# Four graph layers on one core: who writes the edge payload, when partial sums are added, and where masks and table rows are stored

## The chip, the cores and the metric

The kernel runs on one core of a Trainium2 chip. The core has five engines with a queue of instructions each: PE (TensorE, matrix products; its weight loads are listed as PEld), DVE (VectorE), ACT (ScalarE), POOL (GpSimd) and SP (SyncE, which here only issues DMAs). Sixteen DMA engines move data between the core's memory (SBUF, and PSUM for PE's results) and the chip's main memory. The metric is the device time of one launch in microseconds (us), as the median of the runs.

## The reference

The input is 3125 nodes with 32 features, 103,125 directed edges (50,000 pairs both ways and one loop per node, sorted by target), and two vectors per edge. Four layers, each with a layer norm and a ReLU ahead of it and its input added behind it, are applied in turn:

- L0: attention over the edges with four heads, where the softmax of each source node subtracts that source's maximum over its edges;
- L1: two mean aggregations with dense weights;
- L2: a mixture of three Gaussians of the edges' two-vectors;
- L3: a spline network, which takes most of the time and is what the change is about.

```python
def spline_conv(x, row, col, basis, idx, W, b):
    N = x.shape[0]
    Fout = W.shape[2]
    z = jnp.einsum('ni,kio->nko', x, W).reshape(N * K, Fout)
    gathered = z[col[:, None] * K + idx]
    msg = jnp.einsum('es,eso->eo', basis, gathered)
    out = jax.ops.segment_sum(msg, row, num_segments=N)
    deg = jax.ops.segment_sum(jnp.ones_like(msg[:, 0]), row, num_segments=N)
    return out / jnp.maximum(deg, 1.0)[:, None] + b
...
h = jnp.ones((N, 1), x.dtype)
h = jax.nn.elu(spline_conv(h, row, col, basis, idx, stn1_w, stn1_b))
h = jax.nn.elu(spline_conv(h, row, col, basis, idx, stn2_w, stn2_b))
h = jax.nn.elu(h @ stn3_w + stn3_b)
t = h @ stn4_w + stn4_b
new_pseudo = jnp.clip(pseudo + t[col] - t[row], 0.0, 1.0)
basis2, idx2 = spline_basis(new_pseudo)
return spline_conv(x, row, col, basis2, idx2, conv_w, conv_b)
```

There are K = 125 weight matrices in a 5 x 5 x 5 grid, and each edge takes the eight corners of the cell that its three-vector falls into, with eight weights. The first spline layer has an input of ones, so it needs only each source node's sum of corner weights for the 125 grid points. L0 needs, for its maximum and its softmax, the number of edges between each source and each target: a table of counts of 3200 by 3200, mostly zeros.

## The kernel before

**Tiles of edges.** Nodes come in 25 chunks of 128. Edges are put into tiles of 128 edges with sources of one chunk; 24 chunks have 35 tiles each, the last has 15, so there are 855. As the input is sorted by target, tile k of any chunk holds a narrow window of target chunks. The 24 tiles of one k form a unit, and units form groups (`Places`, L884). The line `cuts` (L932) cuts the 35 units into eight groups: 0-2, 2-5, 5-10, 10-15, 15-20, 20-25, 25-29, 29-35. A group has a `need` (the number of input tiles after which it is complete), a `hi` (the last target chunk it reaches) and the flag `counted` (L935): counted groups have their edges counted in the edge stage, the others later, beside the gathers. Of the eight, the first six are counted and the last two are not.

**Edge stage.** The input's 806 tiles are read in 31 blocks of 26. `put_edges` (L1554) loads a block's fields (`flds`), has VectorE compute the payload of each edge (`pay`: 8 fields, the corner weights at L1207 to L1211, the 125 grid weights with the product at L1579, and a column of ones), with two copies by ScalarE (L1562 for the fields, L1583 for the ones), and then has POOL issue 26 indirect DMAs (L1585), each of which scatters 128 payload rows to their places in a table in main memory, `tab`. `pay` has three buffers.

Once a group's rows have landed, its steps run (`group_steps`, L1638, and `add_tiles`, L1596): every third step loads the tiles of three sources back (`tt`, SyncE), and each step is one source of the group: a one-hot of the sources by VectorE (L1374), one matmul per tile into the accumulator `acc1` (L1626), and the addition to `sums` by VectorE (L1628; the first time a copy by ScalarE, L1631). In a counted group, `count_edges` (L1482) then makes a one-hot of the targets per tile by VectorE (`od`, L1381, four buffers), multiplies with the sources' one-hot on PE (`cn`, L1496), and adds what an earlier group left in a column (`carry`, L1512 on VectorE; L1514, a copy by ScalarE, where there is none). Columns that are final go to `a_s`, are stored to `as_d` by SyncE (L1520), turned on PE (L1527), copied by ScalarE (L1528) and stored to `at_d` (L1529). At a group's end its narrow fields (`nar`, one buffer) are stored and its table rows computed.

A loop over the blocks sets the order of the trace: the payload of a block, then a quota of steps of the groups that have come due two blocks after their `need`. What is left after the last block runs one group after the other.

**First gather stage** (L1824 to L1858). For each of 25 chunks: the hidden features (`ps` L1841, `hid`), their transposed copy `hts`, and `spline_rows` (L1432), which makes the chunk's rows of the table z2: 16 pairs of matmuls (`z_ps` L1445, three PSUM buffers), copied into `slab` by ScalarE (L1457 and L1459) and stored by SyncE, four stores a chunk (L1461). Then the groups whose `hi` is this chunk are gathered (`summed_rows`, L1679): per source a one-hot, and per tile one indirect DMA by POOL (L1690, six buffers `g`), a product with the eight corner weights by VectorE (`prod`, L1694), and a matmul into `acc` (L1695, one PSUM buffer). After a source's last tile, VectorE adds the eight corners up (L1702) and adds the result to the total (L1703).

Beside this, `beside` runs steps of another generator, `node_steps` (L1719): each source grants 0.8 us per tile to it, and a step has a price written by hand. It counts the groups that were not counted, the last chunk's edges, prepares L0, and finds the maximum: for each third of the targets and each source chunk it loads the counts (`cnt`, SyncE, L1801), has ScalarE turn them into a mask `off` (L1803: a large number where there is no edge) and has VectorE take four maxima (L1806); `cnt` and `off` have two buffers each. When a pool of buffers is opened over memory that earlier pools used, its tiles wait until those pools are done.

**After that** come L0's attention, L1, L2, the new weights (the np stage) and the **last gather stage** with a second table z3, which uses the same `spline_rows` and `summed_rows`, with the first slab slot copied by VectorE (L1457), two accumulators and nothing beside.

Instructions of one engine are put in order by a scheduler that goes by priorities; `keep_in_program_order` adds an order edge from the instruction traced before it on that engine, and no wait.

## Time and profile before

The times below are of the device; the profiled execution is one run apart from the three.

| what | value |
|---|---|
| runs | 7129.87, 7144.23, 7144.03 us, median 7144.03 |
| profiled execution | 7107.32 us, its span 7105.1 us, mean granted TensorE clock 0.748 |
| busy in the span | PE 61%, PEld 32%, DVE 62%, ACT 23%, POOL 40% |
| stages in the span | places of edges to 170 us; scatters to 1634; remaining add steps to 1830; first gather at 1914.6, first gather stage to 3775; L0 to 4610, L1 to 4790, L2 to 5370, np to 5680; last gather stage to 7105 |
| gathers (L1690) | 1710, POOL 1921.3 us busy, 1124 ns mean |
| scatters (L1585) | 806, POOL 894.2 us busy, 1109 ns mean |
| payload product (L1579) | 5676 to 5704 ns on VectorE, one per block |

A row of a waits view names the waiting engine and its line, then the engine and line that released it, the total, the number of waits and the longest. In a view by stretch each engine has its busy time and the number of its instructions in brackets, followed by the granted clock, the DMA engines' busy share and their rate.

### The profile page before, as it was taken

The page shows a single profiled execution, that of the slowest core. Times are in us where ns is not written, and L with a number is a line of the kernel's source. Part 1 is how long each engine was busy: PE and PEld are TensorE (multiplying, and loading weights), DVE is VectorE, ACT ScalarE, POOL GpSimd, SP SyncE. Part 2 cuts the span into 40 slices and gives each one's busy share as a digit, 9 for nine tenths or more (in the row PEclk, how much of TensorE's full clock was granted, in tenths as well). Part 3 has the DMA queues.
Part 4 walks back from the last instruction along what each step waited for, and adds up shares of the span by engine and source line. Part 5 has one row for each costly group of instructions (what it writes and reads, how often), then busy time and mean ns, then how long its engine had stood idle before and what let it go on. Part 6 is the DMA issues. An engine that isn't in the chain of part 4 may idle for free. (4 is left out here: it accounts for less than half of the span.)

```text
span 7105.1 us, 67076 instructions
## 1 busy us (share of the span) xinstructions
PE 4311.1 (61%) x20956; PEld 2240.6 (32%) x20956; DVE 4426.9 (62%) x8893; ACT 1661.1 (23%) x2860; POOL 2826.5 (40%) x2541
## 2 busy tenths in 40 slices
PE   4023134136788877776777777756775499654445
PEld 1012023125433323222222222255664433333333
DVE  5325255256486686779668989818998955444444
ACT  0012022023424223321205878701110022000000
POOL 0775754741153553646571000000000035677776
PEclk5555566568899787878898999977885556677776
DMA  3123233235698886977864433361114478655543
GB/s 100 51 80 93 73 105 108 76 106 166 253 343 316 310 297 242 366 268 269 332 223 151 119 116 120 107 218 60 54 54 179 147 292 300 200 160 157 156 142 101
DMA packets 524310, 1245.13 MB, mean 175 GB/s; under 512 B 271284, under 2 KB 334463, under 8 KB 510886
## 3 DMA queue, kind: packets, MB, share of 16 engines
q0 software_dynamic: 148912, 613.60, 26.2%
q1 hardware_dynamic: 357974, 613.44, 25.5%
q10 hardware_dynamic: 17056, 13.70, 0.6%
q8 instruction: 168, 2.75, 0.2%
q14 instruction: 200, 1.64, 0.1%
HBM read 907.51 MB, written 366.91 MB: 179 GB/s over the span
## 5 line engine op out<-in xcount | busy, mean ns | idle before, releaser
L1690 POOL DMA_INDIRECT g<-z,base x1710 | 1921.3, 1124 | 1428.3 <-DVE prod L1694 416.1
L1695 PE MATMUL acc<-prod,oh 128*128 128x512 f32 (+1 forms) x3420 | 1633.0, 614 | 828.4 <-DVE prod L1694 487.4
L1695 PEld LDWEIGHTS acc<-prod,oh 128*128 128x128 f32 x3420 | 734.0, 237 | 1747.9 <-issue 971.5
L1585 POOL DMA_INDIRECT tab<-pay,slot x806 | 894.2, 1109 | 604.4 <-issue 396.2
L2152 POOL MEMSET g<- 128x448 f32 x5 | 2.1, 473 | 1895.1 <-PE t_ps L2125 1895.1
L1694 DVE TENSOR_TENSOR prod<-g,w 128x512 f32<-128x512 f32 x855 | 575.7, 688 | 273.5 <-DMA g<-z,base 219.8
L1381 DVE TENSOR_SCALAR od<-iota_n,ends 128x512 bf16<-128x512 int16 (+5 forms) x1721 | 519.0, 355 | 319.1 <-remote 150.4
L1626 PE MATMUL acc<-tt,oh 128*128 128x126 f32 x1710 | 305.3, 324 | 665.7 <-DVE oh L1374 305.5
L1960 PE MATMUL acc<-wt,hx 128*33 128x416 f32 (+1 forms) x1600 | 579.1, 514 | 139.1 <-DVE wt L1958 123.2
L1626 PEld LDWEIGHTS acc<-tt,oh 128*128 128x128 f32 x1710 | 267.6, 227 | 701.4 <-issue 358.5
L1374 DVE TENSOR_TENSOR oh<-iota_f,ends 128x640 f32<-128x640 f32 (+4 forms) x591 | 430.0, 730 | 56.0 <-remote 42.0
L1702 DVE TENSOR_REDUCE part_sum<-acc 128x64 f32<-128x512 f32 (+1 forms) x344 | 191.2, 556 | 438.7 <-remote 228.1
L1694 DVE TENSOR_TENSOR prod<-g,w8n 128x256 f32<-128x256 f32 x855 | 338.4, 421 | 196.6 <-PE acc L1695 74.5
L1806 DVE CUSTOM_DVE_ANT_0 junk<-adr,off 128x1024 f32<-128x1024 f32 (+1 forms) x300 | 379.2, 1264 | 84.8 <-ACT off L1803 48.4
L1496 PE MATMUL cn<-od,oh 128*128 128x256 bf16 (+3 forms) x1411 | 283.1, 331 | 212.1 <-issue 94.0
L1445 PE MATMUL z_ps<-wk,hts 64*128 64x512 f32 (+1 forms) x800 | 400.4, 785 | 16.9 <-ACT slab L1459 11.3
L1459 ACT COPY slab<-z_ps 128x512 f32<-128x512 f32 (+11 forms) x575 | 298.9, 542 | 340.8 <-DVE slab L1457 240.6
L1954 DVE SCALAR_TENSOR_TENSOR low<-rows,bias_d,low 128x1664 f32<-128x1664 f32 (+1 forms) x200 | 368.3, 1882 | 11.1 <-ACT low L1953 11.1
L1958 DVE SCALAR_TENSOR_TENSOR wt<-low,cnt 128x1664 f32<-128x1664 f32 (+1 forms) x200 | 357.3, 1819 | 15.3 <-PE acc L1960 7.0
L1953 ACT ACTIVATE low<-rows,bias_d 128x1664 f32<-128x1664 f32 (+1 forms) x200 | 324.4, 1628 | 65.6 <-DVE wt L1958 45.2
L1960 PEld LDWEIGHTS acc<-wt,hx 128*33 128x33 f32 x1600 | 171.2, 113 | 518.1 <-issue 334.0
L1956 ACT ACTIVATE low<-low 128x1664 f32<-128x1664 f32 (+1 forms) x200 | 306.9, 1537 | 59.6 <-DVE low L1954 59.5
(350 smaller groups left out, 4979.7 us busy)
## 6 DMA issues: line engine op xcount, KB each, us to landing
z<-slab SPq DMA_DIRECT2D x100, 1600.0 KB
z<-slab SPq DMA_DIRECT2D x100, 800.0 KB
lob<-lorow_d SPq DMA_DIRECT2D x70, 768.0 KB
cnt<-at_d SPq DMA_DIRECT2D x100, 416.0 KB
cnt<-as_d SPq DMA_DIRECT2D x50, 800.0 KB
cnt<-at_d SPq DMA_DIRECT2D x100, 384.0 KB
tt<-tab SPq DMA_DIRECT2D x32, 1072.5 KB
g<-z,base POOLq DMA_INDIRECT x1710
```

What stands on the lines that cost most here:

```text
L1374: nc.vector.tensor_tensor(dst_tile[:, :n, :], iota[:, None, :].to_broadcast([P, n, P]), lows[:, :, None].to_broadcast([P, n, P]), OP.is_equal)
L1381: nc.vector.tensor_scalar(dst_tile[:, :w], iota_n[:, lo * P : lo * P + w], ends[:, 1, t : t + 1], None, op0=OP.is_equal)
L1445: nc.tensor.matmul(ps[:, k - k0 : k - k0 + n, :].rearrange("p r f -> p (r f)"), vt[g * fin : (g + 1) * fin, :], wk[g * fin : (g + 1) * fin ...
L1585: put = nc.gpsimd.indirect_dma_start(out=tab, out_offset=bass.IndirectOffsetOnAxis(ap=slot[:, t0 + k : t0 + k + 1], axis=0), in_=pay[:, k, ...
L1626: nc.tensor.matmul(acc[:, : K3 + 1], oh[:, k, :], mine[:, k, i, NAR:], start=(k == 0), stop=(k == m - 1))
L1690: nc.gpsimd.indirect_dma_start(out=g, out_offset=None, in_=table[:rows], in_offset=bass.IndirectOffsetOnAxis(ap=base[:, t : t + 1], axis=0 ...
L1694: nc.vector.tensor_mul(prod, corners(g, fout), w8_of(t).to_broadcast([P, 2, 4, fout]))
L1695: nc.tensor.matmul(acc, oh[:, i, :], prod.rearrange("p j c f -> p (j c f)"), start=(i == 0), stop=(i == n - 1))
L1806: nc.vector.tensor_tensor_reduce(junk, adr[:, hd, :], off, 1.0, -BIG, OP.subtract, OP.max, top[:, j, s, hd : hd + 1])
L1954: nc.vector.scalar_tensor_tensor(low, rows[0], bias_d[:, 0, d, hd : hd + 1], low, op0=OP.add, op1=OP.max)
L1958: nc.vector.scalar_tensor_tensor(wt, low, 1.0, cnt, op0=OP.min, op1=OP.mult)
L1960: nc.tensor.matmul(acc[:, i, :q], hx[:, d, :], wt[:, i * q : (i + 1) * q], start=(d == 0), stop=(d == NCH - 1))
```

## The change

The diff has these parts:

- **Payload.** The two ScalarE copies in `put_edges` become a copy and a memset on VectorE; the tile `ones` goes, and the tile of empty rows holds 5 instead of 6.
- **Sums and carries.** `count_edges` no longer adds the carries itself but returns a function that does (`add_counts`). In the edge stage a step's sum and carries are traced after the next step (`behind`, `finish_sums`), and the VectorE additions among them are kept in program order.
- **Masks.** Where final counts are stored, ScalarE also makes the mask (`a_off`, BF16, one buffer) and SyncE stores it to a new table `off_d`. The maximum loads the mask straight from there, with four buffers.
- **Table stores.** The four stores of a chunk's `slab` are issued by ScalarE, in both gather stages.
- **Add-up.** In `summed_rows` the eight corners of a source are added up after the third product of the next source, kept in program order; each source grants 0.9 instead of 0.8 us per tile.
- **Pools.** The first gather stage's pools wait tile by tile for the memory they reuse, and are opened in another order; `acc` has two PSUM buffers instead of one, `z_ps` two instead of three.
- **Groups.** The cuts become 0-2, 2-5, 5-10, 10-15, 15-20, 20-25, 25-28, 28-32, 32-35: nine groups, of which the first five are counted. The group 20-25 is now counted beside the gathers.
- **End of the edge stage.** `nar` has two buffers, and after the last block the first two open groups run their steps in turn.

The core of the diff:

```diff
         reg = [u for u in self.units if u.t0 < self.tail]
-        late = next(i for i, u in enumerate(reg) if u.need == reg[-1].need)
-        cuts = [0, 2] + list(range(5, late - 2, 5)) + [late, len(reg)]
+        cuts = [0, 2] + list(range(5, len(reg) - 9, 5)) + [len(reg) - 7, len(reg) - 3, len(reg)]
         self.regular_groups = [Group(reg[a:b]) for a, b in zip(cuts, cuts[1:])]
         for g in self.regular_groups:
-            g.counted = g.need + 3 * BLK <= -(-n_edges // P)
+            g.counted = g.need + 5 * BLK <= -(-n_edges // P)
...
                     if r0 + n == Q:
-                        nc.sync.dma_start(view[c, i - 1], slabs.pop(i - 1).rearrange("p r i f -> p (r i f)"))
+                        nc.scalar.dma_start(view[c, i - 1], slabs.pop(i - 1).rearrange("p r i f -> p (r i f)"))
...
                                  start=(i == spans[b][0]), stop=(i == spans[b][1]), skip_group_check=True)
+
+        def finish():
+            add_counts(s, cols, cn, tps)
+        return finish
+
+    def add_counts(s, cols, cn, tps):
...
             to = a_s[:, k * P : m * P] if final else old
             if had:
-                nc.vector.tensor_add(to, new, old)
+                tc.keep_in_program_order(nc.vector.tensor_add(to, new, old))
...
             return
-        nc.sync.dma_start(as_d[s][:, lo * P : (lo + ended) * P], a_s[:, : ended * P])
-        turn_counts(s, lo, ended, a_s, tps)
-
-    def turn_counts(s, lo, n, a_s, tps):
+        counts_out(s, lo, ended, a_s, tps)
+
+    def counts_out(s, lo, n, a_s, tps):
+
+        nc.sync.dma_start(as_d[s][:, lo * P : (lo + n) * P], a_s[:, : n * P])
+        off = cn_a.tile([P, 8 * P], BF, name="a_off", bufs=1)
+        nc.scalar.activation(off[:, : n * P], a_s[:, : n * P], AF.Relu, bias=big, scale=-BIG)
+        nc.sync.dma_start(off_d[s][:, lo * P : (lo + n) * P], off[:, : n * P])
...
             cell, hat = cells(nc, small_p, pos, n)
-            nc.scalar.copy(pay[:, :, 0:8].rearrange("p t f -> p f t"), at)
+            nc.vector.tensor_copy(pay[:, :, 0:8].rearrange("p t f -> p f t"), at)
...
                 w15[:, 2, None, :, :].to_broadcast([P, KS * KS, KS, n]))
-            nc.scalar.copy(pay[:, :, ROW - 1 :], ones[:, :n, None])
+            nc.vector.memset(pay[:, :, ROW - 1 :], 1.0)
...
+
+        def finish_sums(s, acc, counts):
+            if s in summed:
+                tc.keep_in_program_order(nc.vector.tensor_add(sums[:, s, :], sums[:, s, :], acc[:, : K3 + 1]))
+            else:
+                summed.add(s)
+                nc.scalar.copy(sums[:, s, :], acc[:, : K3 + 1])
+            if counts:
+                counts()
+
+        open_steps = []
+
+        def behind(finish):
+
+            open_steps.append(finish)
+            if len(open_steps) > 1:
+                open_steps.pop(0)()
...
                     nc.tensor.matmul(acc[:, : K3 + 1], oh[:, k, :], mine[:, k, i, NAR:], start=(k == 0), stop=(k == m - 1))
-                if s in summed:
-                    nc.vector.tensor_add(sums[:, s, :], sums[:, s, :], acc[:, : K3 + 1])
-                else:
-                    summed.add(s)
-                    nc.scalar.copy(sums[:, s, :], acc[:, : K3 + 1])
+                counts = None
                 if g.counted:
                     ohb = cn_a.tile([P, GK, P], BF, name="oh3")
                     nc.scalar.copy(ohb[:, :m], oh[:, :m])
-                    count_edges(g, s, ohb, cps, tps)
+                    counts = count_edges(g, s, ohb, cps, tps)
+                behind(lambda s=s, acc=acc, counts=counts: finish_sums(s, acc, counts))
...
             n = g.n
-            nar = pool.tile([P, NAR, GT], F32, name="nar", bufs=1)
...
                         pass
-        for *_, steps in todo:
-            for _ in steps:
-                pass
+
+        rest = [steps for *_, steps in todo]
+        while rest:
+            for steps in rest[:2]:
+                if next(steps, rest) is rest:
+                    rest.remove(steps)
+        for finish in open_steps:
+            finish()
         assert put == tr
...
         rows = (grp.hi + 1) * P * ZR
+        last = []
+
+        def add_up(s, acc):
+            v = acc.rearrange("p (c f) -> p f c", c=8)
+            if s not in first:
+                first.add(s)
+                tc.keep_in_program_order(nc.vector.tensor_reduce(total[:, s, :], v, AX.X, OP.add))
+            else:
+                part_sum = pool.tile([P, fout], F32, name="part_sum")
+                tc.keep_in_program_order(nc.vector.tensor_reduce(part_sum, v, AX.X, OP.add))
+                nc.vector.tensor_add(total[:, s, :], total[:, s, :], part_sum)
...
                 nc.vector.tensor_mul(prod, corners(g, fout), w8_of(t).to_broadcast([P, 2, 4, fout]))
                 nc.tensor.matmul(acc, oh[:, i, :], prod.rearrange("p j c f -> p (j c f)"), start=(i == 0), stop=(i == n - 1))
-            v = acc.rearrange("p (c f) -> p f c", c=8)
-            if s not in first:
-                first.add(s)
-                nc.vector.tensor_reduce(total[:, s, :], v, AX.X, OP.add)
-            else:
-                part_sum = pool.tile([P, fout], F32, name="part_sum")
-                nc.vector.tensor_reduce(part_sum, v, AX.X, OP.add)
-                nc.vector.tensor_add(total[:, s, :], total[:, s, :], part_sum)
+                if last and i == min(2, n - 1):
+                    add_up(*last.pop())
+            last.append((s, acc))
             if beside:
-                beside(0.8 * n)
+                beside(0.9 * n)
+        for q, t in last:
+            add_up(q, t)
...
                         onehots(oh, iota_b, low_ends(0, s, g.units[0].tiles[s][1], m), m)
-                        count_edges(g, s, oh, cps, tps)
+                        count_edges(g, s, oh, cps, tps)()
...
                 nc.scalar.copy(a_s[:, :w], cn.rearrange("p b c -> p (b c)")[:, :w])
-                nc.sync.dma_start(as_d[s][:, c0 * P : c0 * P + w], a_s[:, :w])
-                turn_counts(s, c0, c1 + 1 - c0, a_s, tps)
+                counts_out(s, c0, c1 + 1 - c0, a_s, tps)
...
             q = w // 4
-            with tc.tile_pool(name=f"mx{j}", bufs=2, side="right") as pool, tc.tile_pool(name=f"mx{j}c", bufs=1, side="right") as once, \
+            with tc.tile_pool(name=f"mx{j}", bufs=4, side="right") as pool, tc.tile_pool(name=f"mx{j}c", bufs=1, side="right") as once, \
...
                         nc.scalar.copy(adr[:, hd, i * q : (i + 1) * q], ps[:, :q])
                 for s in range(NCH):
-                    cnt = pool.tile([P, w], F16, name="cnt")
-                    nc.sync.dma_start(cnt, as_d[s][:, c0 * P : c0 * P + w])
-                    off = pool.tile([P, w], F32, name="off")
-                    nc.scalar.activation(off, cnt, AF.Relu, bias=big, scale=-BIG)
+                    off = pool.tile([P, w], BF, name="off")
+                    nc.sync.dma_start(off, off_d[s][:, c0 * P : c0 * P + w])
...
 
-    with tc.tile_pool(name="s2c", bufs=1) as once, tc.tile_pool(name="s2", bufs=2) as pool, \
-            tc.tile_pool(name="s2z", bufs=3) as zp, tc.tile_pool(name="s2g", bufs=GB) as gp, \
-            tc.tile_pool(name="s2p", bufs=3) as pp, tc.tile_pool(name="s2_acc", bufs=1, space=PSUM) as psa, \
-            tc.tile_pool(name="s2_ps", bufs=1, space=PSUM) as pst, tc.tile_pool(name="s2_z", bufs=3, space=PSUM) as zps:
+    early = dict(reuse_waits="tile")
+    with tc.tile_pool(name="s2c", bufs=1, **early) as once, tc.tile_pool(name="s2g", bufs=GB, **early) as gp, \
+            tc.tile_pool(name="s2p", bufs=3, **early) as pp, tc.tile_pool(name="s2", bufs=2, **early) as pool, \
+            tc.tile_pool(name="s2z", bufs=3, **early) as zp, tc.tile_pool(name="s2_acc", bufs=2, space=PSUM, **early) as psa, \
+            tc.tile_pool(name="s2_ps", bufs=1, space=PSUM, **early) as pst, \
+            tc.tile_pool(name="s2_z", bufs=2, space=PSUM, **early) as zps:
```

More of the change, by code (lines that the diff above doesn't have):

```diff
@@ L1311, in tile_gnn_places @@
     as_d = [dram.tile([P, NPAD], F16, name=f"as_d{s}") for s in range(NCH)]
+    off_d = [dram.tile([P, NPAD], BF, name=f"off_d{s}") for s in range(NCH)]
     at_d = dram.tile([NCH, P, NPAD], F16, name="at_d")
@@ L1497, in count_edges @@
                                  start=(i == spans[b][0]), stop=(i == spans[b][1]), skip_group_check=True)
+        def finish():
+            add_counts(s, cols, cn, tps)
+        return finish
+    def add_counts(s, cols, cn, tps):
+        lo, width = cols[0][0], len(cols)
         a_s = cn_a.tile([P, 8 * P], F16, name="a_s")
@@ L1541, in tile_gnn_places @@
         nc.sync.dma_start(slot, slot_d)
-        ones = once.tile([P, BLK], F32, name="ones")
-        nc.vector.memset(ones, 1.0)
-        EM = 6
+        EM = 5
         empty = once.tile([P, EM, ROW], F32, name="empty")
@@ L1639, in group_steps @@
             n = g.n
-            nar = pool.tile([P, NAR, GT], F32, name="nar", bufs=1)
+            nar = pool.tile([P, NAR, GT], F32, name="nar", bufs=2)
             if g.t0 < pl.tail:
```

## The prediction

> **What bounds the kernel now.** The span and the table of slices come first: 7105.1 us, no engine above 62%, POOL at five to seven tenths in the first quarter and again in the middle and at the end, and idle in the third quarter. A share of 62% says nothing of a kernel with stages, so the next view is busy time by stretch.
>
> ```profile
> core 0: us, PE busy (x) PEld busy (x) DVE busy (x) ACT busy (x) POOL busy (x), PEclk, DMA share, GB/s
> 170.00:1634.00 1464.00, 345.96 (x2077) 255.92 (x2078) 588.92 (x1673) 236.21 (x741) 894.01 (x806) 0.59 0.30 86
> 1634.00:1842.00 208.00, 146.20 (x1016) 120.27 (x1017) 140.90 (x449) 63.09 (x224) 2.49 (x4) 0.87 0.59 172
> 1842.00:2750.00 908.00, 747.73 (x2062) 298.68 (x2058) 660.38 (x1340) 291.73 (x646) 436.45 (x367) 0.87 0.86 314
> 2750.00:2850.00 100.00, 87.01 (x170) 35.51 (x171) 36.99 (x84) 60.01 (x149) 1.00 (x1) 0.66 0.56 219
> 2850.00:3775.00 925.00, 672.97 (x1258) 227.98 (x1257) 666.28 (x1160) 158.59 (x319) 585.41 (x488) 0.88 0.81 287
> 5683.00:6110.00 427.00, 413.70 (x770) 154.13 (x771) 220.63 (x520) 95.10 (x200) 191.36 (x183) 0.56 0.79 290
> 6110.00:7105.00 995.00, 496.26 (x1366) 329.35 (x1364) 430.97 (x1100) 0.00 (x0) 707.05 (x673) 0.71 0.51 145
> ```
>
> The reader sees four places that the change touches. **Scatters** (170 to 1634): POOL issues 806 scatters, 31 blocks of 26. One is 0.97 us and 0.30 follows it, 33 us for 26; one per block lasts 5.3 to 6.4 us beside VectorE's payload product L1579 (5.68 us). In front of nine blocks POOL has holes, 323 us in all (the largest 84.7), each ending 0.8 us after that block's L1579; the other 1141 us are 36.8 a block. **Tail** (1634 to 1842): POOL idle, the remaining add steps run. **First gather stage** (1842 to 3775): the z2 table is made in 25 chunks and 855 gathers read it. POOL stands seven times for table rows, 365 us, after 72.3 us ahead of the first gather. **Last gather stage** (5683 to 7105): first PE is at 97% with the matmuls of z, then POOL is near its own rate, 673 gathers in 995 us. The rest, 1908 us from 3775 to 5683, the change leaves as it is but for one group more to loop over.
>
> The waits say whose work the holes are. Between 170 and 1640:
>
> ```profile
> ACT pay L1562 <- DMA tab<-pay,slot: 474.6, 13, 51.5
> POOL tab L1585 <- issue: 396.2, 789, 44.0
> DVE sums L1628 <- remote: 185.4, 16, 31.8
> DVE od L1381 <- remote: 150.4, 30, 14.9
> ```
>
> and between 1830 and 3790:
>
> ```profile
> ACT off L1803 <- DVE top L1806: 413.2, 45, 15.4
> POOL g L1690 <- DMA cnt<-as_d: 218.6, 3, 103.9
> DVE prod L1694 <- DMA g<-z,base: 219.8, 205, 5.3
> POOL g L1690 <- DVE prod L1694: 198.8, 170, 7.9
> PEld acc L1695 <- DVE part_sum L1702: 181.4, 93, 6.2
> PE acc L1695 <- DVE part_sum L1702: 104.7, 82, 5.4
> ```
>
> Columns: engine, its line, what it waited for, total, times, longest. In the first list VectorE stands up to 31.8 us at L1628, which needs PE's result; the next payload is behind it in the same queue. In the second, PE waits 286 us for the sum of the one accumulator, and ScalarE's mask waits for the buffers of the maximum. SyncE's list shows its mask loads (L1801) behind the same buffers 535.9 us, and the table stores (L1461) share that queue.
>
> **The change, part by part** (against the profiled 7107 us).
>
> *Sums and carries behind the next step.* The 16 waits at L1628 and those at L1512 leave the spot in front of the payload. What is late next: od L1381 (150.4 us) keeps its wait for PE through its four buffers, and the add work has to be done somewhere. While POOL scatters, PE's completions come 0.71 per 4 us, while it is idle 6.95; in a quiet stretch a counted step takes 3.05 us. So holes that vanish come back partly as tail. Bounds: nothing (or 30 us lost, one more late payload of the usual size) to 250 of the 323 us. I take 60, near the lower end, as od's row is as large as L1628's.
>
> *Payload by VectorE alone.* ScalarE's copies, 0.55 and 0.24 us, go; VectorE gets two small ones. Nearest rows: 0.20 us (L1211, 26 columns) and 0.51 (L1207, 208), so 0.7 us x 31 = 22 us on an engine busy 589 of 1464; in the holes it delays a payload nine times, 6 us. The wait on ScalarE's 474.6 us row is for a pay buffer, and stays, now on VectorE: with three buffers the payload of a block cannot start before the scatters three blocks back are done; behind it stands all add work. Price: 0 if VectorE reaches it late, as before each hole, up to one scatter block per early payload. Cost taken: +6. The L1579 row shows a VectorE operation stretching a scatter by its own length. [...]
>
> *Cuts and counting.* The group of units 20 to 25 is no longer counted in the edge stage, its 24 steps of counting go to the work beside the gathers. From 1634 to 1723 the trace has 25 counted updates L1628, 3.56 us each; from 1723 to 1830, 47 uncounted, 2.28 each. 24 x 1.28 = 31 us leave the tail. In the gather stage they are 24 x 3.6 us (0.84 one-hot, 5 od of 0.37, 0.9 carries) = 86 us of VectorE. Regular groups go from 8 to 9: 24 more add steps (about 0.5 us fixed, L1628's 0.28 and a start, +12), and 24 more sources in each gather stage, 0.69 + 0.22 us in the first (+22 of VectorE), about 0.6 in the last (+15).
>
> *Two open groups interleaved, `nar` twice.* ScalarE waits for tt loads 65 us of the last 107; VectorE is 61 busy, PE 70. A second group's load hides the first's: -15 (0 to -35, where VectorE and PE would be full).
>
> *Pools by tile.* Between the tail's end and the first gather lie 84 us for chunks 0 to 2, whose PE work is 3 x 18. Their sums are ready as the last group's steps 0 to 2 end, some 20 steps earlier. PE is idle 36 of the 107 us. I take -45 (0, if the buffers are those of the last steps, to -66).
>
> *Masks stored, stores on ScalarE, second accumulator, deferred add_up.* 75 activations of 1.2 us leave the gather stage, and the ScalarE-VectorE ring at L1803/L1806 with them; a mask becomes a load. Some 195 smaller activations (0.3 to 1.0 us by the casts of the same tile) and as many stores go where the counts are made, where ScalarE is 16% busy; SyncE then issues 0.33 us more per step. The mask has one buffer, so an activation waits until the store before it has landed; the nearest landing in the chain of waits is a table store's 4.6 us, against 3.56 us from one counted step to the next in the tail: 0 to 25 x 1 us, with the next carry and tile copies queued behind it on ScalarE. I take 0, since ScalarE is idle half of that stretch. The stores cost SyncE 0.32 us each, so ScalarE pays 4 x 0.32 x 25 = 32 us a stage, of 506 busy in 1923. The second accumulator and the late add_up take PE out of its 286 us. Two z banks for three cost about 2 us a chunk where PE waits for the eviction (0.53 us each), +50 at worst. All these aim at 365 us of holes. Bounds: -250 (PE is busy 1508 of 1933 us and gets about 60 more, so a floor near 1570) to +100. I take a third of the holes, -120, and +40 of the 108 us of new VectorE work, since VectorE is 70% busy here but full in the mixed parts (2.0 us a gather against POOL's 1.33). The Trainium skill, "DMA: Bandwidth & Descriptors", section "Issuing engines are not separate DMA queues", says that another issuer saves its sequencer's time alone; by it this part is worth SyncE's 0.32 us each, nothing, and only the freed order of SyncE's queue could pay.
>
> *Last gather stage.* Its first 427 us are PE's and remain. In the 995 us, 673 x 1.33 = 895 are POOL's; 100 can go at most, and 15 are added. I take -40 net (+30 to -80).
>
> Sum: -60 +6 -31 +12 -15 -45 -120 +40 -40 = -253, so about 6855 profiled. The runs' median is 37 us above this execution: **6890**.
>
> **Rivals.**
> 1. *Holes filled, forecast:* -253. For: each hole ends on a named wait that the change takes away. Chance 0.52.
> 2. *Much more is filled:* scatters -150, gathers -250, last stage -80, tail as above: -510, 6630. For: VectorE 30% and POOL 47% idle in the gather stage; against: PE's floor of 1570. 0.16.
> 3. *Only the front gains:* tail and chunk start -80, holes move but stay, as PE's slow completions beside POOL and VectorE's mixed pace set them: about 7060. 0.15.
> 4. *Slower, VectorE the bound of the first gather stage:* the 86 + 22 us of new work and the later add_up, pinned behind a third product that waits 1 to 5 us for its gather, come in the mixed part, where POOL's gather already waits for VectorE's product (198.8 us); 108 + 50 for the banks + 32 for ScalarE's issues = 190, less 80 at the front: about 7107 + 110 + 37 = 7254. It decides once the holes give back under 110 us. 0.13.
> 5. *The pins do nothing,* as the scheduler had that order: the rest remains, -195, 6950; within the forecast's spread. 0.04.
>
> Measurement tells about 0.2% (14 us) from no change. Faster by more: all of 1, 2 and 5 and most of 3, 0.84; within, 0.03; slower, 0.13. The range runs from the second rival's 6630 to just above the third's, 7130, which leaves out the fourth and a little beneath, some 0.17.
>
> **What would show it.** Right: holes before scatter blocks below 260 us; first gather at about 1780; fewer than 300 us of POOL waiting for table rows; no ScalarE mask rows beside the gathers; PE's wait for part_sum near nothing. Wrong: scatter blocks longer than 37 us, VectorE waiting for pay's buffer, more than 2.0 us a gather in the mixed part, or PE waiting on slab copies. A tail longer than 208 us would say that filled holes were only moved.

## The result and the profile after

The changed kernel takes 7224.97 us (median of four runs, 7211.97 to 7232.96) where the kernel before took 7141.72 in the same comparison: a ratio of 1.0118, 95% interval 1.0098 to 1.0138. It is slower by some 83 us, where 250 us of gain had been forecast. The profiled execution took 7211.97 us, its span is 7210.2 us, 105 more than before, and the mean granted clock 0.731 against 0.748.

The first view is again busy time by stretch, of the changed kernel, cut at the last scatter, at 1842 (where the view before is cut too), at the first gather, the last gather of the first gather stage and the first gather of the last stage:

```profile
core 0: us, PE busy (x) PEld busy (x) DVE busy (x) ACT busy (x) POOL busy (x), PEclk, DMA share, GB/s
173.00:1612.00 1439.00, 392.08 (x2084) 288.04 (x2098) 601.04 (x1726) 281.14 (x804) 884.70 (x806) 0.58 0.35 95
1612.00:1842.00 230.00, 129.24 (x711) 113.85 (x713) 97.09 (x338) 29.72 (x142) 3.99 (x5) 0.74 0.51 130
1842.00:1924.00 82.00, 69.47 (x215) 27.15 (x216) 34.96 (x107) 51.97 (x133) 0.10 (x1) 0.77 0.70 271
1924.00:3889.00 1965.00, 1591.49 (x3543) 550.08 (x3551) 1454.37 (x2849) 484.17 (x1099) 1063.10 (x855) 0.83 0.81 292
5813.00:7210.00 1397.00, 911.22 (x2068) 471.52 (x2065) 652.08 (x1660) 82.06 (x170) 886.88 (x855) 0.66 0.59 184
```

The first gather stage has grown from 1861 to 1965 us, counted from the first to the last gather. The second row ends at 1842 in both kernels, so its 230 us against 208 say only that the last scatter came earlier; the tail is measured by the marks below. From its first to its last gather the last stage is about as long as before (1388 us then). Read against five marks in both traces, to about 1 us, the 105 us come out as follows; the attention's first matmul now comes 111 us before the last product of the stage (17 us after it in the kernel before), so the stage is measured up to the attention's end:

| stretch | before | after | difference |
|---|---|---|---|
| last scatter at | 1634 | 1611 | -23 |
| last scatter to last addition to `sums` | 193 | 220 | +27 |
| from there to the first gather | 87 | 93 | +6 |
| first gather to the end of the attention | 2676 | 2753 | +77 |
| L1, L2, np | 1093 | 1101 | +8 |
| first z3 matmul to the end | 1421 | 1431 | +10 |

Next come the waits; line numbers are those of the kernel that a view belongs to. In the edge stage of the changed kernel:

```profile
POOL tab L1595 <- DVE od L1381: 180.9, 6, 46.0
DVE od L1381 <- remote: 207.2, 47, 26.0
DVE oh L1374 <- remote: 145.0, 21, 15.0
DVE sums L1608 <- remote: 31.7, 3, 22.8
```

VectorE's wait at the sums went from 185 to 32 us, as intended, but the wait went to the next instructions that need PE, the one-hots L1381 (150 before, now 207) and L1374 (42 before over the span, now 145 in this stage): the holes between scatters are 310 us where they were 326. In the gather stage:

```profile
PE acc L1736 <- DVE prod L1735: 247.6, 228, 11.6
PE z_ps L1445 <- ACT slab L1459: 28.6, 25, 3.9
PE ps L1883 <- DVE hid L1882: 25.0, 6, 7.8
```

and of its weight loads (PEld), in the changed kernel and then in the kernel before (1830 to 3790 us):

```profile
PEld acc L1736 <- DVE prod L1735: 589.8, 491, 12.4
```

```profile
PEld acc L1695 <- DVE prod L1694: 365.8, 404, 5.3
PEld acc L1695 <- DVE part_sum L1702: 181.4, 93, 6.2
```

The 99 us that PE's matmuls spent on `part_sum` are gone; but their wait for products is 60 us longer (187 before), that of the weight loads 224, and z_ps now waits 29 us for the eviction where it waited 11. The waits of matmuls and of weight loads overlap in time. With each stretch of time counted once, PE's wait at the accumulator for `part_sum` fell from 182 to 16 us and its wait there for products rose from 437 to 599: PE was released from one wait into another of the same size. The holes over 10 us between gathers grew from 375 to 473 us.

### The profile page after: what moved, and what is told of

Same layout as the page of the kernel before. It is cut to its first block, busy times and chain, and to the rows that moved or that the text cites. A ratio compares the mean times of both kernels' runs of the same rounds, so it can differ in the third digit from the quotient of the medians.

```text
span 7210.2 us, 68160 instructions
## 1 busy us (share of the span) xinstructions
PE 4521.4 (63%) x20874; PEld 2281.7 (32%) x20904; DVE 4517.0 (63%) x9289; ACT 1673.9 (23%) x2940; POOL 2847.0 (39%) x2543
## 5 line engine op out<-in xcount | busy, mean ns | idle before, releaser
L1731 POOL DMA_INDIRECT g<-z,base x1710 | 1950.1, 1140 | 1741.9 <-DVE prod L1735 421.8
L1736 PE MATMUL acc<-prod,oh 128*128 128x512 f32 (+1 forms) x3420 | 1690.3, 623 | 733.6 <-DVE prod L1735 506.3
L1736 PEld LDWEIGHTS acc<-prod,oh 128*128 128x128 f32 x3420 | 719.1, 237 | 1663.1 <-issue 828.9
L1374 DVE TENSOR_TENSOR oh<-iota_f,ends 128x640 f32<-128x640 f32 (+3 forms) x663 | 444.5, 672 | 693.7 <-remote 409.8
L1381 DVE TENSOR_SCALAR od<-iota_n,ends 128x512 bf16<-128x512 int16 (+5 forms) x1721 | 536.0, 357 | 495.0 <-remote 207.2
L1653 PE MATMUL acc<-tt,oh 128*128 128x126 f32 x1710 | 337.7, 359 | 612.3 <-DVE od L1381 248.5
L1445 PE MATMUL z_ps<-wk,hts 64*128 64x512 f32 (+1 forms) x800 | 479.9, 845 | 65.6 <-ACT slab L1459 36.2
L1653 PEld LDWEIGHTS acc<-tt,oh 128*128 128x128 f32 x1710 | 302.7, 261 | 650.3 <-issue 427.4
L1496 PE MATMUL cn<-od,oh 128*128 128x256 bf16 (+3 forms) x1331 | 304.7, 358 | 234.4 <-DVE od L1381 107.3
L1539 PE MATMUL cn<-ident_h,a_s 128*128 128x128 f16 x625 | 98.3, 257 | 336.1 <-DVE a_s L1520 142.7
```

What stands on the lines that cost most here:

```text
L1374: nc.vector.tensor_tensor(dst_tile[:, :n, :], iota[:, None, :].to_broadcast([P, n, P]), lows[:, :, None].to_broadcast([P, n, P]), OP.is_equal)
L1381: nc.vector.tensor_scalar(dst_tile[:, :w], iota_n[:, lo * P : lo * P + w], ends[:, 1, t : t + 1], None, op0=OP.is_equal)
L1445: nc.tensor.matmul(ps[:, k - k0 : k - k0 + n, :].rearrange("p r f -> p (r f)"), vt[g * fin : (g + 1) * fin, :], wk[g * fin : (g + 1) * fin ...
L1653: nc.tensor.matmul(acc[:, : K3 + 1], oh[:, k, :], mine[:, k, i, NAR:], start=(k == 0), stop=(k == m - 1))
L1731: nc.gpsimd.indirect_dma_start(out=g, out_offset=None, in_=table[:rows], in_offset=bass.IndirectOffsetOnAxis(ap=base[:, t : t + 1], axis=0 ...
L1736: nc.tensor.matmul(acc, oh[:, i, :], prod.rearrange("p j c f -> p (j c f)"), start=(i == 0), stop=(i == n - 1))
```

## The experiments

The letters u and b in a label mean one part undone in the changed kernel and one part alone in the kernel before; half_new is the changed kernel with four parts undone. Each ratio is to the kernel before, timed beside it. The kernel before took 7113 to 7120 us beside these runs, except beside half_new, half_store, b_store and b_early, where it took 6855; so these four are compared by ratio and with each other. The runs came in five batches, each on another chip. The table has the stretches from one trace of each kernel (of b_store its fastest execution, 6847 of 6847 to 6907 us), to about 1 us; differences of whole kernels in us are worked out from the ratios (tail: last scatter to first gather; gather: first gather to the end of the attention; last: first z3 matmul to the end).

| kernel | ratio, 95% interval | tail | gather | last |
|---|---|---|---|---|
| before | 1 | 281 | 2676 | 1421 |
| changed; again | 1.0118 (1.0098-1.0138); 1.0098 (1.0063-1.0133) | 313; 310 | 2753; 2743 | 1431; 1436 |
| u_acc | 1.0087 (1.0062-1.0112) | 300 | 2761 | 1412 |
| u_store | 1.0116 (1.0067-1.0164) | 306 | 2702 | 1482 |
| u_counted | 1.0108 (1.0068-1.0149) | 377 | 2687 | 1414 |
| u_tail | 1.0071 (1.0044-1.0097) | 270 | 2773 | 1434 |
| u_mask | 1.0085 (1.0059-1.0111) | 316 | 2719 | 1416 |
| b_cuts | 0.9952 (0.9930-0.9974) | 260 | 2668 | 1399 |
| b_sums | 0.9995 (0.9978-1.0012) | 286 | 2692 | 1417 |
| b_addup | 1.0062 (1.0037-1.0088) | 306 | 2676 | 1457 |
| best_two | 0.9955 (0.9934-0.9975) | 271 | 2666 | 1404 |
| half_again | 0.9979 (0.9959-0.9998) | 258 | 2690 | 1415 |
| half_mask | 0.9949 (0.9933-0.9964) | 247 | 2714 | 1421 |
| half_tail | 1.0045 (1.0016-1.0074) | 298 | 2683 | 1424 |
| by_three | 0.9982 (0.9958-1.0007) | 262 | 2704 | 1425 |
| half_new (beside 6855) | 0.9917 (0.9897-0.9937) | 233 | 2701 | 1371 |
| half_store (beside 6855) | 1.0022 (0.9998-1.0046) | 236 | 2782 | 1332 |
| b_store (beside 6855) | 1.0059 (1.0039-1.0079) | 267 | 2700 | 1313 |
| b_early (beside 6855) | 0.9908 (0.9877-0.9940) | 254 | 2631 | 1351 |

**One part undone.** The first theories: A, two z_ps buffers slow the table down; B, ScalarE's store issues hold its copies; C, the moved counting makes VectorE the bound; T1, two groups in turn take each other's load buffer.

u_acc (one accumulator, three z_ps buffers, add-up at once; its two additions are also no longer kept in program order):

```diff
-name="s2_acc", bufs=2 ... name="s2_z", bufs=2
+name="s2_acc", bufs=1 ... name="s2_z", bufs=3
-                if last and i == min(2, n - 1):
-                    add_up(*last.pop())
-            last.append((s, acc))
+            add_up(s, acc)
```

> The changed kernel, but the first gather stage has one accumulator and three PSUM buffers for z_ps again, and a source's corners are added up right after it. Theory A (the table's matmuls wait for evictions with two buffers: a chunk alone takes 26 to 37 us instead of 18 to 22): a chunk alone falls back to about 20 us, the seven or eight holes in POOL's gathers shrink by 60 to 110 us in all, total about 7130 to 7165. Theory B (ScalarE's store issues hold its evictions): the buffers matter little, total 7200 to 7230, a chunk alone stays near 30 us. Theory C (the moved counting makes VectorE the bound): the total stays or rises, as PE's wait for part_sum returns.

u_store:

```diff
-                        nc.scalar.dma_start(view[c, i - 1], ...
+                        nc.sync.dma_start(view[c, i - 1], ...
```

> The changed kernel, but SyncE issues the table stores again. Theory A: within 20 us of 7225. Theory B: ScalarE gets 32 us a stage back and evictions follow matmuls sooner, 7150 to 7190, a chunk alone 5 to 10 us shorter. Theory C: within 20 us of 7225.

u_counted:

```diff
-            g.counted = g.need + 5 * BLK <= -(-n_edges // P)
+            g.counted = g.need + 3 * BLK <= -(-n_edges // P)
```

> The changed kernel, but the group of units 20 to 25 is counted in the edge stage again (nine groups stay). Theory A: the gather stage gets 20 to 40 us back and the tail loses about 30, total 7205 to 7235. Theory B: the same. Theory C: the gather stage gets 86 us or more of VectorE back, total 7140 to 7175.

u_tail:

```diff
-            for steps in rest[:2]:
+            for steps in rest[:1]:
```

> The changed kernel, but the groups left after the last block run one after the other again. Theory T1 (two groups in turn hold both tt buffers, so that no load runs ahead, and this makes the tail 32 us longer than before): from the last scatter to the first gather falls from 312 us to 240 to 270, total 7160 to 7190. Theory T2 (the tail is longer because more add work was left for it by the edge stage): the stretch stays at 300 or above, total 7215 to 7250.

None gave back more than half, and only u_tail's interval lies clear of the changed kernel's first one; none is clear of the second. In u_acc a chunk made alone (from its first to its last table matmul, with no gather's matmul between) did fall from 25 to 46 us (median 29) to 18 to 25 (median 19), as theory A had it, yet the holes between gathers grew from 473 to 512 us: the table was made faster but later, and the gain that A forecast, 60 us and more, did not come. In u_counted the gather stage got 66 us back and the tail took 64 more, so the move itself is neutral: theory C falls. u_store gained 51 us in the gather stage, where a chunk alone took 21 to 33 us (median 25), in part as theory B has it, and lost as much in the last stage, so that its total did not move. u_tail did what T1 says, 42 us in the tail.

**One part alone.** b_cuts has the two lines of the cuts and of `counted`, b_sums `finish`, `behind` and the two pins in the edge stage, b_addup the pools' buffers and `add_up`, each as in the diff of the change. u_mask is the changed kernel with the mask made from `cnt` again:

```diff
-        off = cn_a.tile([P, 8 * P], BF, name="a_off", bufs=1)
-        nc.scalar.activation(off[:, : n * P], a_s[:, : n * P], AF.Relu, bias=big, scale=-BIG)
-        nc.sync.dma_start(off_d[s][:, lo * P : (lo + n) * P], off[:, : n * P])
...
-                    nc.sync.dma_start(off, off_d[s][:, c0 * P : c0 * P + w])
+                    nc.sync.dma_start(cnt, as_d[s][:, c0 * P : c0 * P + w])
+                    nc.scalar.activation(off, cnt, AF.Relu, bias=big, scale=-BIG)
```

> The kernel before with one part alone: nine groups, the group of units 20 to 25 counted beside the gathers. Theory A (what is lost is lost by the new groups and the moved counting, since VectorE and PE have less slack beside the gathers than in the edge stage): 40 to 90 us slower than the kernel before, with from first gather to the end of the attention 60 to 100 us longer and the tail 10 to 30 shorter. Theory B (the loss is in the new masks, whose single buffer holds ScalarE while PE waits for its evictions): within 25 us of the kernel before.

> The kernel before with one part alone: sums and carries traced behind the next step and kept in program order. As predicted it would gain 60 us. Theory P (PE's completions beside scatters set the pace, the holes only move): scatter holes stay at 290 to 330 us, the last scatter ends within 25 us of 1634, total within 30 us. Rival: the holes fall below 250 us and the total by 40 or more.

> The kernel before with one part alone: two accumulators and two PSUM buffers for z_ps in the first gather stage, and the add-up of a source after the third product of the next, in both gather stages. Theory E (a bank is only moved from the table to the sums): within 25 us; PE's wait for part_sum (286 us) goes, a chunk of the table made alone takes 26 to 30 us instead of 18 to 22. Rival: the freed PE makes the gather stage 40 us or more shorter.

> The changed kernel, but the masks are made from the counts beside the gathers again (no off_d, two buffers). Theory A: within 25 us of the changed kernel. Theory B: from first gather to the end of the attention falls by 50 us or more below the changed kernel's 2753 us, and the total to 1.006 or less of the kernel before.

The new groups gain 34 us, all three stretches shorter: the reverse of what I then held. The pinned sums change nothing that can be told, with 307 us of holes: theory P holds. b_addup loses 44 us, more than the 25 of theory E: the time from the last sum to the first gather is 27 us longer, the gather stage is as long as before, and the last stage, whose buffers are not changed, is 36 us longer. Of these 36, 24 fall in the part where the table z3 is made, with the granted clock at 0.53 where the kernel before had 0.56; so they are not shown to be a cost of the late add-up. u_mask is 24 us nearer, 34 of them in the gather stage, but its interval overlaps the changed kernel's.

The granted clock sets the kernels with two accumulators, two z_ps buffers and the late add-up apart. Over all timed runs they have 0.729 to 0.741, the others 0.740 to 0.759. b_addup has 0.732 to 0.738 where the kernel before, beside it, has 0.742 to 0.749; u_acc, where all three are undone, is back at 0.741 to 0.749. No run separates a lower clock as a cause of the lost time from one that follows from the order of the work.

For b_addup, the row of the matmuls of one chunk made alone, first in the kernel before (2180 to 2203 us), then in b_addup (2221 to 2247 us); the columns are busy time and mean, then the idle time before and what ended it:

```profile
L1445 PE MATMUL z_ps<-wk,hts 64*128 64x512 f32 (+1 forms) x33 | 15.7, 663 | 1.3 <-ACT hts L1848 1.0 <-ACT slab L1459 0.3
L1445 PEld LDWEIGHTS z_ps<-wk,hts 64*128 64x128 f32 x34 | 5.0, 192 | 6.1 <-ACT slab L1459 2.8 <-ACT slab L1457 1.2 <-ACT hts L1848 1.1
```

```profile
L1445 PE MATMUL z_ps<-wk,hts 64*128 64x512 f32 (+1 forms) x37 | 19.8, 777 | 1.7 <-ACT slab L1459 1.6
L1445 PEld LDWEIGHTS z_ps<-wk,hts 64*128 64x128 f32 x36 | 6.5, 222 | 9.5 <-ACT slab L1459 6.4 <-ACT slab L1457 2.6
```

With two buffers the weight load waits 9.0 us a chunk for ScalarE's copies instead of 4.0, and the matmul is modelled longer; the granted clock is 0.80 here and 0.85 in the kernel before. Over all traces, the 159 chunks made alone with three buffers take 19.8 us in the median, the 72 with two 29.2. The clock is only part of this: at 0.70 to 0.80 the medians are 19.7 and 28.3, at 0.50 they are 23.4 and 35.0. It is lower in the second kind: 35 of the 72 ran at 0.50, against 9 of the 159.

**Half of the change.** half_new undoes stores, accumulators with the add-up, masks and the groups in turn (the edits of u_acc, u_store, u_mask and u_tail together). half_store is half_new with ScalarE's stores, b_store and b_early are the kernel before with ScalarE's stores and with the new pools (one accumulator, three z_ps buffers).

> The changed kernel with four parts undone together: accumulators, z_ps buffers and add-up as before, table stores by SyncE, masks made beside the gathers, groups left after the last block one after the other. What stays of the change is the groups, the pinned sums, the payload by VectorE, the pools by tile and 0.9 us per tile. Theory F (the loss lies in these four, together about 100 us, and the new groups gain 34): 7060 to 7110 where the kernel before takes 7120, tail at 170 to 200 us, chunks of the table made beside the gathers again. Theory G (it lies in the pools by tile, the payload or the larger grant): slower than the kernel before by 30 us or more.

> The same kernel as half_new, but with the table stores issued by ScalarE. Theory S (an instruction of ScalarE's queue that waits for a chunk's last copy, and the order that follows from it, push the making of chunks out of the time of the gathers): 30 to 80 us slower than half_new, holes between gathers 80 us or more larger. Rival: the same within 20 us, only 32 us of issues on an engine with slack.

> The kernel before with one part alone: table stores issued by ScalarE. Theory S: 30 to 80 us slower than the kernel before, chunks made alone in POOL's holes. Rival: within 20 us.

> The kernel before with one part alone: the first gather stage's pools wait tile by tile and are opened in the new order (one accumulator, three z_ps buffers). As predicted: first gather 45 us earlier, attention otherwise as before, total 30 to 45 us faster. Theory G: the stretch from first gather to the end of the attention grows by more than that, as the attention's first work is put among the last gathers; total slower.

half_store is 72 us slower than half_new (1.05% of 6855), b_store 40 slower than the kernel before. The reason is not that ScalarE makes a chunk more slowly: a chunk made alone takes 17 to 23 us in half_store and 17 to 27 in half_new. What differs is the place of the chunks in PE's queue. The table has, from the traces, how many gathers have their matmul ahead of the first and of the last table matmul of a chunk.

```
chunk          3        4        5          9          10         13         17         21
half_new     0-8      8-38   120-120    123-133    136-179    243-255    366-371    489-494
half_store  48-48    48-48   120-120    123-163    243-243    243-279    486-486    609-609
before       0-6      8-36    38-60     123-138    142-188    243-248    366-371    489-499
b_store     48-48    48-48    48-84     123-167    183-219    342-363    409-435    489-509
changed      0-32    34-48    48-84     123-165    166-215    243-291    366-385    489-509
u_store      0-14    15-42    44-66     123-137    141-184    243-256    366-376    489-500
u_acc       48-48    48-48   120-120    243-243    243-243    243-278    366-381    489-504
```

48 gathers are all of the first group. In half_new chunk 3 is made while they run; in half_store all 48 stand ahead of it, and POOL, done with them, waits for the chunk. It shows as POOL's waits, in half_new and then in half_store, over the gather stage:

```profile
POOL g L1728 <- DMA at_d<-a_t: 311.2, 2, 227.9
POOL g L1728 <- DMA z<-slab: 51.4, 2, 27.3
```

```profile
POOL g L1728 <- DMA as_d<-a_s: 509.4, 5, 229.8
POOL g L1728 <- DMA z<-slab: 94.2, 1, 94.2
```

Each first row holds the wait ahead of the first gather (its longest); the names are of the store that the profile saw last, while each of these holes ends with the stores of the chunk that is gathered next. Without the first wait the holes between gathers are 386 and 552 us. In the changed kernel the chunks are partly pushed back too, with two buffers and ScalarE's stores together; u_store moves them forward again and has 370 us of holes instead of 473, and u_acc, whose chunks are fast, has them as late as half_store. That the order makes the loss is read from these orders and waits: no run kept ScalarE's stores and put the chunks back in their places. Why the scheduler, given a store on ScalarE, puts a chunk last was not followed further.

In the last stage the kernels with the same stores are shorter: 1332 against 1371, and 1431 against 1482 with SyncE (u_store). The clock in the part where z3 is made differs too, 0.60 against 0.52 and 0.58 against 0.50, and u_acc, with ScalarE's stores and the add-up at once, has 1412 where kernels with SyncE's stores have 1399 to 1425 on other chips; so a gain by the stores is not shown. No kernel had ScalarE's stores in the last stage alone.

**The rest.** half_mask and half_tail each add one part to half_new; best_two is b_cuts and b_early together; after_again is the changed kernel.

> The changed kernel once more, to have it on one chip with the next three. If the parts add up on every chip: 1.008 to 1.015 of the kernel before. Rival (the edge stage of the chip decides): within 0.4% of it where the scatters are faster.

> The kernel before with two parts: the nine groups with the moved counting (0.9952 alone) and the pools by tile in the new order (0.9908 alone). If they are independent: 0.986. Rival (both live from the same slack beside the gathers): no better than 0.991.

> half_new (0.9917) with one part added: the masks are made and stored with the counts, one buffer. Theory B (the single buffer holds ScalarE, and the table's copies queue behind it): 0.995 or more. Theory A: 0.989 to 0.994. As predicted: 0.985 or less.

> half_new (0.9917) with one part added: after the last block the first two groups run step by step in turn. Theory T1 (both tt buffers are held, no load runs ahead): the stretch from the last scatter to the first gather grows by 25 to 50 us, 0.995 to 0.999. As predicted: 15 us shorter, 0.990.

by_three lets each group keep its turn for a whole load; half_again is half_new.

```diff
             for steps in rest[:2]:
-                if next(steps, rest) is rest:
-                    rest.remove(steps)
+                for _ in range(SB):
+                    if next(steps, rest) is rest:
+                        rest.remove(steps)
+                        break
```

> half_tail, but the two groups change over after three steps, that is, when a tt load has been used up, so that the second buffer is free for the next load meanwhile. Theory T1 (both buffers held): VectorE's wait for tt between the last scatter and the sums' end falls from 85 us to below 60, that stretch from 219 us to 150 to 180, the total to 0.990 to 0.996 of the kernel before. Rival (changing over itself, or the second nar, costs): the stretch stays above 200 us and the total above 1.000.

> half_new once more, groups left one after the other: stretch from the last scatter to the sums' end 150 to 170 us, total 0.990 to 0.996 of the kernel before.

The wait that T1 names is there. VectorE's waits between the last scatter and the last sum, in half_tail, by_three and half_again:

```profile
DVE ends L1640 <- DMA tt<-tab: 85.0, 25, 11.6
```

```profile
DVE ends L1640 <- DMA tt<-tab: 56.8, 20, 15.4
```

```profile
DVE ends L1640 <- DMA tt<-tab: 52.8, 26, 11.0
```

Two groups step by step hold both `tt` buffers for six steps, and no load runs ahead; the stretch is 219, 184 and 178 us. Changing over by loads shortens it by 35 us, though by_three and half_again stayed above the 0.990 to 0.996 that was expected of them. Even then by_three is no faster than one group after the other (0.9982, 0.9979): no gain is left to be seen. The masks can't be told from nothing: half_mask is 0.9949 against half_again's 0.9979, on another chip and with intervals that overlap, and undoing them in the changed kernel gave 24 us, also with intervals that overlap.

half_new and half_again are one kernel, and their ratios, 0.9917 and 0.9979, differ by more than both intervals: from one chip to another a ratio can move by 0.6%. So b_early's 0.9908, measured on the chip of half_new's 0.9917, may hold some of that. best_two is faster than both kernels, by 32 us against the kernel before (its ratio; the medians are 43 us apart), but no faster than b_cuts, so on that chip the gain of the pools did not come on top: its attention begins after the last product (18 us), while in b_early, which counts the group 20-25 in the edge stage, it begins 376 us before. That this is why was not tried.

## Why the prediction was wrong, point by point

- **The step that failed** is "I take a third of the holes, -120" for masks, stores, accumulator and add-up in the first gather stage. With the +40 for new VectorE work the sum has -80 there; the stage measured +77, and the holes between gathers grew from 375 to 473 us. Two of these parts cost where a gain was entered: the accumulator with its banks and the late add-up +44 alone (b_addup), stores on ScalarE +72 and +40 in two pairs. In the changed kernel itself undoing the stores moved the total by nothing (1.0116 against 1.0118): 51 us gained in the gather stage were lost in the last one.
- **Stores on ScalarE** I took as 32 us on an idle engine. I never costed the place of the table's chunks in PE's queue: the order of instructions is built anew with each edit, and which chunk runs beside which gathers is part of it. That the order carries the loss is argued from orders and waits, not shown by a run. The Trainium skill ("DMA: Bandwidth & Descriptors", section "Issuing engines are not separate DMA queues") says that another issuer saves only the time to issue; no run speaks against that for the transfers, but the kernels differed by 40 to 72 us.
- **The 286 us of waiting at the accumulator** were misread. They add PE's matmuls (104.7) and its weight loads (181.4), which wait at the same time; counted once they are 182 us. They fell to 16, and PE's wait there for products grew by 162: freeing the accumulator only moved the wait.
- **The bank for the accumulator.** "About 2 us a chunk" was too small: a chunk made alone takes 27.4 us in b_addup where the kernel before has 19.6 (medians), and about 9 us more at a like clock over all traces; the time ahead of the first gather grew by 27 us. The lower granted clock of these kernels was in no term.
- **Two groups in turn**, taken as -15, cost 40 to 42 us of tail: I counted the loads that a second group could hide and not the two buffers that both groups share.
- **Sums behind the next step**, -60: nothing (0.9995). The condition that I named, od keeps its wait, is what happened, and more: od's wait marked "remote" went from 150 us to 306 in b_sums.
- **Cuts and counting**: the sum gave -31 +12 in the tail and about +40 and +15 in the gather stages; alone it is -34 us, with 21, 8 and 22 us less in tail, gather stage and last stage. The 22 are not shown to come from the groups: half_again and half_mask have the same groups and the last stage's code of b_cuts, and 1415 and 1421 us there against 1399. Where the counting is done is neutral to 2 us between gather stage and tail, as 31 us were priced out of the tail and 64 came.
- **Pools by tile**, -45 ahead of the first gather: from the last sum to the first gather b_early has 84 us and best_two 85 where the kernel before has 87, so this mechanism gave about 3 us. b_early is faster, 0.9908, but because its gather stage is shorter (2631 against 2676, with the attention begun early); that its total is near the forecast is luck.
- **Payload on VectorE**: not tried alone. The Trainium skill ("SBUF — State Buffer", section "Who interferes with whom") names VectorE's copies among the operations that can take the port pair shared with GpSimd. Here 20 of the 28 scatters that ran beside the new copy took 1.03 us or less, where the median of all is 0.97, and scatters above 1.5 us were 24 where they were 26 before: no cost of that kind is seen.
- **Last gather stage**, -40: +10. What the stores and the late add-up do there is open, as the granted clock differs in each pair.
- **The signs that I named**: holes before scatters stayed at 310 us (below 260 was forecast), the first gather came at 1924 (1780), POOL's holes grew; only the wait for `part_sum` and the mask rows made from `cnt` beside the gathers went as forecast. Of the signs of being wrong, a longer tail and PE waiting on slab copies came; VectorE's wait for pay's buffer, 182 us, had been 263 before.
- Rival 4 gave the sign and the place, the first gather stage, at 7254; its mechanism, moved counting on VectorE, was refuted by b_cuts. So the sign was covered and the cause was not, though its 50 us for the banks point at a part that did cost.

The parts alone (b_cuts -34, b_sums 0, b_addup +44, b_store +40, two groups in turn +47 by half_tail against half_again, b_early between 0 in best_two and -63) add to between +34 and +97; the change measured +69 to +83. They were measured on different chips, so this sum is rough. How the remaining difference is shared among payload, masks and the larger grant stays open.

## What to carry to other kernels

A wait in a profile is a gain only if nothing else is late behind it: ask what the freed engine meets next, and check the order in its queue. Waits of PE's matmuls and of its weight loads overlap; don't add them. Where a scheduler orders an engine's instructions, any edit can reorder them; compare the order of the built kernels before pricing instructions. Before two streams of work are interleaved or a buffer is moved from one to the other, count the buffers that each needs to run one load ahead.

## What the runs showed of the hardware

The same kernel can meet a different edge stage. half_new and half_again are one kernel; the last scatter came at 1423 us in one and 1629 in the other, with the same 0.97 us per scatter. VectorE's waits over the edge stage, first in half_again:

```profile
DVE pay L1569 <- DMA tab<-pay,slot: 319.6, 15, 27.3
DVE od L1381 <- remote: 228.5, 32, 35.7
DVE oh L1374 <- remote: 77.3, 9, 29.5
```

and in half_new:

```profile
DVE pay L1569 <- DMA tab<-pay,slot: 408.0, 18, 28.9
DVE a_s L1520 <- DMA as_d<-a_s: 84.3, 13, 18.1
DVE od L1381 <- PE cn L1496: 67.8, 27, 49.3
```

The waits marked "remote", on PE's completions beside POOL's scatters, are absent in the second, and the holes between scatters are 66 instead of 305 us. The kernel is the same, so the slow completions of this stage belong to where or when it ran: the two runs were made on different chips at different times, and don't say which of the two it is.
